# ScalarE's layer evictions move behind the next step's count eviction

## The chip, the cores and the metric

The kernel runs on one core of a Trainium2 chip. Its time is the device time of one execution in microseconds. The engines are named as in the profile: PE is TensorE's matmuls and PEld its weight loads, ACT is ScalarE, DVE is VectorE, POOL is GpSimd, SP is SyncE. Each engine runs its own instructions in their written order, and the engines wait for one another through signals (semaphores).

## What is computed

A wide-and-deep recommender for 16384 rows: mean word embeddings of 32 tokens, mean embeddings of three features of 20 ids each, four single ids, a wide sum, and a network of three layers with ReLU.

```python
tok = word_emb[token_idx].mean(axis=1)
e1 = emb_mh1[mh1_idx].mean(axis=1)
...
o4 = emb_oh4[oh4_idx]
emb = jnp.concatenate([tok, e1, e2, e3, o1, o2, o3, o4], axis=1)
...
h = jax.nn.relu(emb @ W1 + b1)
h = jax.nn.relu(h @ W2 + b2)
h = jax.nn.relu(h @ W3 + b3)
return jax.nn.sigmoid(h @ Wd + bd + wide)
```

The layers are 748 to 1024, to 512, to 256, and to 1.

## The kernel before

The batch is cut into 128 tiles of 128 rows. A tile takes 11 steps (`STEPS`), and the main loop (L528) runs over all steps, 1408 and 16 more at the end for what is left (`WAKE`). The order of the work on every engine is the order in which this loop writes it.

**Counts.** The small features are not gathered. DVE makes one-hot rows of the ids (`one_hots`, L291; tiles `row` and `slice`), for the step after the current one. PE multiplies them in `counts` (L307): 12 matmuls a step, 8 in a tile's last, into the PSUM tile `pc`, of which there is one. ACT evicts `pc` into `cnt` (L324). PE can't start the next step's counts before that eviction has ended.

**Sums.** In the tile after, `small_sums` (L332) multiplies `cnt` with the tables: some 15 matmuls a step into `pg`, right behind the step's counts. DVE reduces `pg` into `g` (L348).

**Tokens.** POOL gathers the word embeddings, two rows of each batch row at a time (`tokens`, L222; tile `tok_rows`, 8 buffers), 4096 indirect transfers. DVE adds them up (`add_up`, L210; lines L214 to L220). POOL can issue the next gather into a buffer when DVE has added the one before.

**Transposes.** When a tile's sums or tokens are complete, PE transposes them (`add_small`, L380, and `add_tokens`, L394) into a PSUM tile `pt`, and DVE copies `pt` into the layers' input. In the loop the transposes stand right behind the step's counts.

**Layers.** `mlp` (L432) runs on two tiles of rows at a time. Each layer's output is cut into tiles of 128 columns: `layer` (L414) adds up one such tile in PSUM (`ph`) with 6, 8 or 4 matmuls, and ACT evicts it with ReLU into `h` (L428). At the end come the output row `po` (L444) and the sigmoid. `mlp` is a generator: at each step's end `Paced.to` (L461) takes from it as many matmuls as are due, about four. So a `ph` may be begun in one step and finished in another, and the step that finishes one often begins the next. `ph`, `pt`, `po` and `pk` (the transposed ids, L282) share two PSUM buffers (`ps_h`); a new tile takes the buffer that was given back first.

A step writes its work in this order: one-hots, counts and their eviction, transposes, token adds, sums, layers.

Of the kernel before, what the change touches and what calls it, by code (L numbers as in the profile page):

```python
# [13 lines left out]
AF = mybir.ActivationFunctionType  # L14
# [17 lines left out]
STEPS = -(-HALF // ONEHOT)  # L32
# [16 lines left out]
def kernel(  # L49
# [21 lines left out]
    nc = tc.nc  # L71
# [7 lines left out]
    for f in SMALL:  # L79
        n = -(-tables[f].shape[0] // P)  # L80
# [210 lines left out]
    def one_hots(sc, s, i):  # L291

        b = i * ONEHOT
        rows = min(ONEHOT, HALF - b)
        row1 = ohp.tile([P, ONEHOT, P], BF16, name="row1")
        slice1 = ohp.tile([P, ONEHOT, n_h], BF16, name="slice1")
        for w, (one, n) in enumerate(((row1, P), (slice1, n_h))):
            shape = [P, rows, n // 2, 2]
            nc.vector.tensor_tensor(  # L299
                one[:, 0:rows, :].rearrange("p i (n d) -> p i n d", d=2),  # L300
                iota[:, 0:n].rearrange("p (n d) -> p n d", d=2).unsqueeze(1).to_broadcast(shape),
                sc[:, s // 2, w, s % 2, b : b + rows, :].unsqueeze(2).to_broadcast(shape),
                ALU.is_equal,
            )
        return row1, slice1

    def counts(cnt, hot, i):  # L307

        b = i * ONEHOT
        rows = min(ONEHOT, HALF - b)  # L310
        n = rows // 2
        pc = ps_c.tile([P, 2, 2, 512], F32, name="pc")
        for k in range(rows):
            for f in range(2):
                half = slice(f * HALF, (f + 1) * HALF)
                at = k % n * n_h
                nc.tensor.matmul(  # L317
                    pc[:, f, k // n, at : at + n_h],
                    hot[0][half, k, :],
                    hot[1][half, k, :],  # L320
                    start=True,
                    stop=True,
                )
        nc.scalar.activation(  # L324
            cnt[:, :, b : b + rows, :].rearrange("l f (g k) h -> l f g (k h)", g=2),
            pc[:, :, :, 0 : n * n_h],
            AF.Copy,
            scale=0.5,
            saturate=False,
        )  # L330
# [36 lines left out]
    class Block:  # L367
# [42 lines left out]
        def chunk(self, k):  # L410
            x = self.small[:, k, :] if k < 4 else self.tok[:, k - 4, :]
            return x[: chunk_k[k], 0 : self.n]

    def layer(dst, weights, bias, srcs, n_out):  # L414
        n = srcs[0].shape[-1]
        for m in range(n_out):
            ph = ps_h.tile([P, N], F32, name="ph", tag="ph")
            for k, src in enumerate(srcs):
                nc.tensor.matmul(  # L419
                    ph[:, 0:n],  # L420
                    weights[: src.shape[0], k, m * P : (m + 1) * P],
                    src,
                    start=(k == 0),
                    stop=(k == len(srcs) - 1),
                )
                if k < len(srcs) - 1:
                    yield 1
            nc.scalar.activation(dst[:, m, 0:n], ph[:, 0:n], AF.Relu, bias=bias[:, m : m + 1])  # L428
            yield 1
        yield None  # L430

    def mlp(block):  # L432


        n = block.n
        h1 = hp.tile([P, M1, N], F32, name="h1", tag="odd")
        yield from layer(h1, w1_sb, b1_sb, [block.chunk(k) for k in range(NK)], M1)
        h2 = hp.tile([P, M2, N], F32, name="h2", tag="even")
        yield from layer(h2, w2_sb, b2_sb, [h1[:, k, 0:n] for k in range(M1)], M2)
        h3 = hp.tile([P, M3 + 1, N], F32, name="h3", tag="odd")  # L440
        yield from layer(h3, w3_sb, b3_sb, [h2[:, k, 0:n] for k in range(M2)], M3)
        po = ps_h.tile([1, N], F32, name="po", tag="ph")
        for k in range(M3):
            nc.tensor.matmul(  # L444
                po[:, 0:n], wd_sb[:, k : k + 1], h3[:, k, 0:n], start=(k == 0), stop=(k == M3 - 1)
            )
        y = h3[0:1, M3, 0:n]
        nc.vector.tensor_add(y, po[:, 0:n], block.wide[:, 0:n])
        nc.scalar.activation(y, y, AF.Sigmoid, bias=bd_sb)
        b0 = block.first * P  # L450
        nc.sync.dma_start(out=out[b0 : b0 + n, :].rearrange("n o -> o n"), in_=y)
        yield M3
# [44 lines left out]
    tiles = B // P  # L497
# [26 lines left out]
    tables_on_chip = Paced(tables_on_chip)  # L524
    sc = key_columns(lookup_keys(ix))
    hot = one_hots(sc, 0, 0)
    layers, before, g = None, None, None
    for step in range(n_steps):  # L528
        t, i = divmod(step, STEPS)
        s = t % NSUB  # L530
        if i == 0:
            if g is not None:
                wide_term(g)
                waiting.append((step + 1, Block.add_small, t - 2, g))
            sums = g = None
            if 1 <= t <= tiles:
                g = gp.tile([P, G_COLS], F32, name="g")
                sums = sums_by_step(small_sums(g, cnt))
            if t < tiles:
                if s == 0 and t:  # L540
                    sc = next_sc
                cnt = cp.tile([P, 2, HALF, n_h], FP8, name="cnt", tag="counts")
        if t < tiles:
            hot_now = hot
            if s == 1 and i == 0 and t + NSUB < tiles:
                ix = load_indices(t // NSUB + 1)
            if s == 2 and i == 0 and t + NSUB < tiles + 1:
                next_keys = lookup_keys(ix)
            if i < STEPS - 1:
                hot = one_hots(sc, s, i + 1)  # L550
            elif t + 1 < tiles:
                hot = one_hots(next_sc if s == NSUB - 1 else sc, (s + 1) % NSUB, 0)
            counts(cnt, hot_now, i)
            tables_on_chip.to(TABLE_PACE * (step - 2))
            if t == 1 and i == STEPS - 1:
                load_weights()
        if waiting and step >= waiting[0][0]:
            block = transpose(*waiting.pop(0)[1:])
            if block:
                if layers:  # L560
                    layers.finish()
                layers = Paced(mlp(block), LAYER_TIME * block.n / P)
                last = block.first + block.n // P
                begin, left = step, (ready(ends[last] - 1) if last < tiles else n_steps) - step
        known = set(sums_of)
        toks.to(n_all * (step + 1) / n_steps)
        for k in set(sums_of) - known:
            waiting.append((step + 2, Block.add_tokens, k, sums_of.pop(k)))
        if s == 2 and i == 1 and t + NSUB < tiles + 1:
            next_sc = key_columns(next_keys)  # L570
        ahead = 0
        if sums:
            done = next(sums)
            ahead = n_h * (i + 1) / STEPS - done
        if layers:
            layers.to(mlp_work * layers.size * (step + 1 - begin) / left + ahead)
# [43 lines left out]
```

## Time and profile before

| | before |
|---|---|
| median of 3 runs (lowest to highest) | 7639.67 us (7632.0 to 7650.83) |
| the profiled execution | 7640.41 us, span 7638.6 us |
| mean granted clock of TensorE | 0.875 |
| busy share PE, PEld, DVE, ACT, POOL | 78%, 61%, 51%, 34%, 51% |

In the rows of the profile a number behind `x` counts instructions. In a timeline row stand the start in the span, the busy time, the engine, line and operation, what it writes and reads, and in brackets how long the engine was idle before and what ended that. In a row of waits stand who waited for whom, the total, how many times, and the longest. `remote` is a wait that no instruction in the trace ends, and `issue` is time in which the engine waited for nothing that the profile shows. In a row of windows stand the stretch, its length, the busy time of each engine with its instructions, the granted clock, the share of DMA and GB/s. In a group's row stand the busy time, the mean in ns, and the idle time before.

### The profile page before, as it was taken

Reading aid. Unit: us, or ns where it says so; the run is one execution under the profiler, and the core shown is the slowest. Engines: PE = TensorE matmul, PEld = TensorE weight load, DVE = VectorE, ACT = ScalarE, POOL = GpSimd, SP = SyncE. Lnnn points to the kernel's source line nnn. Section 1 sums busy time; section 2 is a strip of 40 time slices with the busy share of each in tenths; the row PEclk is TensorE's granted clock in tenths of the full one; section 3 lists DMA queues with packets and bytes.
Section 4 is the critical chain, followed back from the end, with each engine's and each line's share of the span. In section 5 each row is a group of like instructions: output and inputs, shape, how many; then the busy total and the mean of one; then the engine's idle time right before and its main releaser. Section 6 shows DMA issues by size and latency. Waiting matters only on the chain.

```text
span 7638.6 us, 116204 instructions
## 1 busy us (share of the span) xinstructions
PE 5965.6 (78%) x46772; PEld 4692.2 (61%) x46772; DVE 3907.9 (51%) x8513; ACT 2574.7 (34%) x2403; POOL 3887.3 (51%) x4103
## 2 busy tenths in 40 slices
PE   4777777877777787877888888777778777777778
PEld 3656666666656666666666666666666666666667
DVE  6544454455544555545555555555545545454543
ACT  4333333333333333333333333333333333333332
POOL 6544454454554455555555555555555545444543
PEclk8888888888988888888888889898888988888889
DMA  5333333333333333333333333333333333333322
GB/s 147 86 81 84 82 84 82 83 86 82 84 84 83 82 86 86 83 86 84 88 88 85 88 87 90 88 86 86 87 85 86 87 81 83 81 81 82 85 80 64
DMA packets 253003, 653.37 MB, mean 86 GB/s; under 512 B 119040, under 2 KB 119617, under 8 KB 252461
## 3 DMA queue, kind: packets, MB, share of 16 engines
q0 software_dynamic: 196608, 629.41, 30.4%
q1 hardware_dynamic: 55853, 16.53, 1.0%
q8 instruction: 366, 6.00, 0.3%
q14 instruction: 176, 1.44, 0.1%
HBM read 645.59 MB, written 0.07 MB: 85 GB/s over the span
## 4 chain that ended last, share of the span: by engine, by line
PE 52%; another core or an unknown queue 19%; DVE 14%; issue 11%; ACT 4%; DVEq 0%; SPq 0%; DMA 0%; ACTq 0%
PE ph L419 24%; PE pg L342 17%; PE pc L317 8%; DVE own L216 4%; ACT cnt L324 4%; DVE slice L299 3%; DVE own L220 3%; DVE row L299 1%; PE po L444 1%; PE pt L387 1%; ACT h L428 1%; PE pt L403 1%; DVE g L348 0%; PE pt L384 0%
## 5 line engine op out<-in xcount | busy, mean ns | idle before, releaser
L232 POOL DMA_INDIRECT tok_rows<-in_word_emb_dram,it x4096 | 3886.4, 949 | 3711.7 <-DVE own L220 2388.0
L324 ACT ACTIVATE cnt<-pc 128x1656 fp8e3<-128x1656 f32 (+1 forms) x1408 | 2123.6, 1508 | 3163.7 <-remote 1568.4
L342 PE MATMUL pg<-terms,cnt 128*128 128x195 bf16 x17664 | 2187.3, 273 | 454.9 <-issue 394.1
L342 PEld LDWEIGHTS <-cnt 128*128 128x128 fp8e3 x17664 | 1805.4, 147 | 730.6 <-issue 612.7
L299 DVE TENSOR_TENSOR row<-own,sc 128x768 bf16<-128x768 bf16 (+1 forms) x1408 | 763.1, 542 | 1828.6 <-remote 1349.5
L317 PE MATMUL pc<-slice,row 64*128 64x138 bf16 x16384 | 824.6, 236 | 865.6 <-ACT cnt L324 336.1
L419 PE MATMUL ph<-h,w_sb 128*128 128x256 f32 (+1 forms) x5200 | 1395.8, 411 | 97.6 <-issue 90.4
L317 PEld LDWEIGHTS <-row 64*128 64x128 bf16 x16384 | 575.3, 100 | 1373.0 <-issue 1183.0
L419 PE MATMUL ph<-x_small,w_sb 128*128 128x256 f32 (+3 forms) x4160 | 1203.8, 418 | 85.2 <-issue 66.3
L419 PEld LDWEIGHTS ph<-h,w_sb 128*128 128x128 f32 x5200 | 1021.8, 210 | 277.9 <-issue 146.7
L428 ACT ACTIVATE h<-ph,b_sb 128x256 f32<-128x256 f32 (+1 forms) x910 | 427.6, 470 | 1813.5 <-remote 859.3
L419 PEld LDWEIGHTS ph<-x_small,w_sb 128*128 128x128 f32 (+1 forms) x4160 | 827.1, 213 | 236.9 <-issue 120.4
L216 DVE TENSOR_TENSOR own<-own,tok_rows 128x300 f32<-128x300 f32 x1920 | 917.0, 478 | 63.1
L348 DVE TENSOR_REDUCE g<-pg 128x130 f32<-128x390 f32 (+1 forms) x512 | 261.5, 511 | 1232.2 <-remote 515.9
L220 DVE TENSOR_TENSOR own<-own,tok_rows 128x300 f32<-128x300 f32 x1792 | 857.1, 478 | 61.8
L299 DVE TENSOR_TENSOR slice<-own,sc 128x828 bf16<-128x828 bf16 (+1 forms) x1408 | 797.0, 566 | 0.0
L419 PE MATMUL ph<-x_tok,w_sb 128*128 128x256 f32 (+1 forms) x2080 | 624.6, 407 | 23.1 <-issue 22.2
L419 PEld LDWEIGHTS ph<-x_tok,w_sb 128*128 128x128 f32 x2080 | 409.9, 209 | 88.0 <-issue 36.6
L405 DVE TENSOR_SCALAR x_tok<-pt 128x256 f32<-128x256 f32 x128 | 54.3, 424 | 338.3 <-PE pt L404 269.3
L388 DVE TENSOR_TENSOR x_small<-pt,scale 128x384 f32<-128x384 f32 x128 | 70.9, 554 | 104.3 <-PE pt L387 84.3
L444 PE MATMUL po<-h,wd_sb 128*1 128x256 f32 (+1 forms) x260 | 89.3, 470 | 37.4 <-ACT h L428 25.4
L403 PE MATMUL pt<-ident,g_tok 128*128 128x128 f32 x256 | 59.8, 316 | 28.1 <-ACT h L428 22.5
(43 smaller groups left out, 805.4 us busy)
## 6 DMA issues: line engine op xcount, KB each, us to landing
tok_rows<-in_word_emb_dram,it POOLq DMA_INDIRECT x4096
ix<-in_idx_dram SPq DMA_DIRECT2D x128, 32.0 KB
w_sb<-in_W_dram SPq DMA_DIRECT2D x6, 512.0 KB
raw<-in_mh_dram SPq DMA_DIRECT2D x3, 747.5 KB
it<-in_idx_dram SPq DMA_DIRECT2D x32, 64.0 KB
w_sb<-in_W_dram SPq DMA_DIRECT2D x1, 2048.0 KB
out_dram<-h SPq DMA_DIRECT2D x63, 1.0 KB
raw<-in_mh_dram SPq DMA_DIRECT2D x1, 617.5 KB
```

Of the source, the lines that this page charges most:

```text
L216: nc.vector.tensor_add(tok_sum, tok_sum, a)
L220: nc.vector.tensor_add(to, tok_sum, b)
L232: nc.gpsimd.indirect_dma_start(out=rows[:, r * TOK_D : (r + 1) * TOK_D], out_offset=None, in_=word, in_offset=bass.IndirectOffsetOnAxis(ap ...
L299: nc.vector.tensor_tensor(one[:, 0:rows, :].rearrange("p i (n d) -> p i n d", d=2), iota[:, 0:n].rearrange("p (n d) -> p n d", d=2).unsque ...
L317: nc.tensor.matmul(pc[:, f, k // n, at : at + n_h], hot[0][half, k, :], hot[1][half, k, :], start=True, stop=True,)
L324: nc.scalar.activation(cnt[:, :, b : b + rows, :].rearrange("l f (g k) h -> l f g (k h)", g=2), pc[:, :, :, 0 : n * n_h], AF.Copy, scale=0 ...
L342: nc.tensor.matmul(pg[:, j, :], by_slice[:, :, h], terms[:, h, :], start=(h == h0), stop=(h == h1 - 1))
L348: nc.vector.tensor_reduce(g[:, at : at + n * ROW].rearrange("p (f d) -> p f d", f=n), pg[:, 0:n, :].rearrange("p f (c d) -> p f d c", c=3) ...
L403: nc.tensor.transpose(pt[:, k, :], g[:, k * P : (k + 1) * P], ident)
L419: nc.tensor.matmul(ph[:, 0:n], weights[: src.shape[0], k, m * P : (m + 1) * P], src, start=(k == 0), stop=(k == len(srcs) - 1),)
L428: nc.scalar.activation(dst[:, m, 0:n], ph[:, 0:n], AF.Relu, bias=bias[:, m : m + 1])
L444: nc.tensor.matmul(po[:, 0:n], wd_sb[:, k : k + 1], h3[:, k, 0:n], start=(k == 0), stop=(k == M3 - 1))
```

## The change

A finished layer tile is no longer evicted at once. `evict_later` notes it, and `evict` writes the noted eviction behind the next step's count eviction. It is written earlier where another tile is finished before that, so that at most one is noted; where a layer has ended and the generator goes on; and at the end, once all counts are written. Since PE runs in order, a count eviction that has waited for its counts has waited for every layer matmul ahead of them as well, and the layer's eviction behind it needs no signal of its own: of PE's 3259 instructions that signal, 2397 are left. The matmuls keep their order and number on PE, and so does the work of DVE, POOL and SP.

```diff
--- before.py
+++ after.py
@@ -411,6 +411,21 @@
             x = self.small[:, k, :] if k < 4 else self.tok[:, k - 4, :]
             return x[: chunk_k[k], 0 : self.n]
 
+    unevicted = []
+
+    def evict():
+        for dst, ph, bias in unevicted:
+            nc.scalar.activation(dst, ph, AF.Relu, bias=bias)
+        unevicted.clear()
+
+    def evict_later(*what):
+
+
+        evict()
+        unevicted.append(what)
+        if counted == tiles:
+            evict()
+
     def layer(dst, weights, bias, srcs, n_out):
         n = srcs[0].shape[-1]
         for m in range(n_out):
@@ -425,9 +440,10 @@
                 )
                 if k < len(srcs) - 1:
                     yield 1
-            nc.scalar.activation(dst[:, m, 0:n], ph[:, 0:n], AF.Relu, bias=bias[:, m : m + 1])
+            evict_later(dst[:, m, 0:n], ph[:, 0:n], bias[:, m : m + 1])
             yield 1
         yield None
+        evict()
 
     def mlp(block):
 
@@ -524,7 +540,7 @@
     tables_on_chip = Paced(tables_on_chip)
     sc = key_columns(lookup_keys(ix))
     hot = one_hots(sc, 0, 0)
-    layers, before, g = None, None, None
+    layers, g, counted = None, None, 0
     for step in range(n_steps):
         t, i = divmod(step, STEPS)
         s = t % NSUB
@@ -551,6 +567,8 @@
             elif t + 1 < tiles:
                 hot = one_hots(next_sc if s == NSUB - 1 else sc, (s + 1) % NSUB, 0)
             counts(cnt, hot_now, i)
+            evict()
+            counted = t + (i == STEPS - 1)
             tables_on_chip.to(TABLE_PACE * (step - 2))
             if t == 1 and i == STEPS - 1:
                 load_weights()
```

The lines from L414 on move by 15 to 18; the layer's eviction is L418, the layer's matmul L434 and the output row's L460. What stands on ACT at one place in the middle of the program, the first layer of a block (`h1` from `ph` is a layer's eviction, `cnt` from `pc` a count eviction; the numbers tell the tiles apart and shift by one in the changed kernel; in brackets whose signals an instruction waits for), before:

```order
L324 ACTIVATE cnt_19669<-pc_20145 128x2x552 [waits PE_49]
L428 ACTIVATE h1_19772<-ph_20135,b1_sb_133 128x256 [waits PE_49]
L324 ACTIVATE cnt_20175<-pc_20180 128x2x828 [waits PE_49]
L428 ACTIVATE h1_19772<-ph_20165,b1_sb_133 128x256 [waits PE_49]
L324 ACTIVATE cnt_20175<-pc_20232 128x2x828 [waits PE_49]
L428 ACTIVATE h1_19772<-ph_20224,b1_sb_133 128x256 [waits PE_49]
L324 ACTIVATE cnt_20175<-pc_20283 128x2x828 [waits PE_49]
```

and after the change:

```order
L324 ACTIVATE cnt_19668<-pc_20144 128x2x552 [waits PE_49]
L418 ACTIVATE h1_19772<-ph_20056,b1_sb_133 128x256
L324 ACTIVATE cnt_20174<-pc_20179 128x2x828 [waits PE_49]
L418 ACTIVATE h1_19772<-ph_20134,b1_sb_133 128x256
L324 ACTIVATE cnt_20174<-pc_20231 128x2x828 [waits PE_49]
L418 ACTIVATE h1_19772<-ph_20164,b1_sb_133 128x256
L324 ACTIVATE cnt_20174<-pc_20282 128x2x828 [waits PE_49]
```

Every layer eviction has moved behind one more count eviction and has lost its wait for PE: that of `ph_20165` stood ahead of the eviction of `pc_20232`, and as `ph_20164` it stands behind that of `pc_20231`, the same tile.

What stands on PE at that place, from the end of these counts to the first sums, before:

```order
L317 LDWEIGHTS row1_20176
L317 MATMUL pc_20232<-slice1_20177,row1_20176 128x138
L384 MATMUL pt_20246<-ident_103,g_19668 128x128 [waits Activation_49]
L387 MATMUL pt_20246<-ident_103,g_19668 128x128 x3
L342 LDWEIGHTS cnt_19669
L342 MATMUL pg_20259<-terms_128,cnt_19669 128x195 [waits DVE_49]
```

and after the change:

```order
L317 LDWEIGHTS row1_20175
L317 MATMUL pc_20231<-slice1_20176,row1_20175 128x138
L384 MATMUL pt_20246<-ident_103,g_19667 128x128 [waits Activation_49]
L387 MATMUL pt_20246<-ident_103,g_19667 128x128 x3
L342 LDWEIGHTS cnt_19668
L342 MATMUL pg_20259<-terms_128,cnt_19668 128x195 [waits DVE_49]
```

PE's rows are the same, and nothing has moved on it. The transpose waits for ACT in both, since it takes the buffer of the layer tile that was finished just ahead of these counts (`ph_20165`, now `ph_20164`). But the eviction that gives this buffer back now stands behind the eviction of the counts right above the transpose.

## The prediction

> **What bounds the kernel now.** I read the page first, then the waits by engine, then single steps in order of time.
>
> ```profile
> span 7638.6 us, 116204 instructions
> PE 5965.6 (78%) x46772; PEld 4692.2 (61%) x46772; DVE 3907.9 (51%) x8513; ACT 2574.7 (34%) x2403; POOL 3887.3 (51%) x4103
> PE 52%; another core or an unknown queue 19%; DVE 14%; issue 11%; ACT 4%; DVEq 0%; SPq 0%; DMA 0%; ACTq 0%
> ```
>
> TensorE (PE) looks like the bound, but 19% of the chain is time that no instruction of another engine ends, on a kernel of one core. Two stretches of the trace show that PE's work alone doesn't set the pace. The first pair of rows counts the count matmuls (128 per batch tile), the second all engines.
>
> ```profile
> 117.10:172.70 55.60, 7.61 (x128) 16.60 (x11) 0.71 0.34 92
> 231.80:7500.00 7268.20, 789.22 (x15804) 2047.89 (x1358) 0.88 0.31 84
> 117.10:172.70 55.60, 29.71 (x277) 24.68 (x277) 31.77 (x72) 16.60 (x11) 30.33 (x33) 0.71 0.34 92
> 231.80:7500.00 7268.20, 5733.01 (x44886) 4495.50 (x44886) 3727.44 (x8130) 2451.22 (x2280) 3700.21 (x3911) 0.88 0.31 84
> ```
>
> In the first stretch no layer runs yet: one tile takes 55.6 us with PE busy for 29.7. Afterwards 7268.2 x 128 / 15804 = 58.9 us per tile, with PE busy for 5733.0 x 128 / 15804 = 46.4: 16.7 us more PE work costs 3.3 (the granted clock was 0.71 and 0.88, so the work differs by rather more). So something else has the larger say. The waits:
>
> ```profile
> ACT cnt L324 <- remote: 1568.4, 292, 12.1
> ACT h L428 <- remote: 859.3, 153, 12.1
> POOL tok_rows L232 <- DVE own L220: 2388.0, 666, 17.1
> PE pc L317 <- ACT cnt L324: 336.1, 142, 10.4
> ```
>
> ScalarE (ACT) waits 1568 us for counts and 859 us for layers with no visible end. One such place, in order of time:
>
> ```profile
> 5672.13 0.54 PE L317 MATMUL pc<-slice,row 64*128 64x138 bf16 x12
> 5673.55 0.94 POOL L232 DMA_INDIRECT tok_rows<-in_word_emb_dram,it  x1 [0.30 <-issue]
> ...
> 5674.60 0.09 PEld L317 LDWEIGHTS <-row 64*128 64x128 bf16 x1 [0.33 <-issue]
> ...
> 5678.55 0.95 POOL L232 DMA_INDIRECT tok_rows<-in_word_emb_dram,it  x1 [0.30 <-issue]
> 5680.23 1.55 ACT L324 ACTIVATE cnt<-pc 128x1656 fp8e3<-128x1656 f32 x1 [9.76 <-remote]
> ...
> 5681.76 0.47 ACT L428 ACTIVATE h<-ph,b_sb 128x256 f32<-128x256 f32 x1
> 5681.83 0.88 PE L317 MATMUL pc<-slice,row 64*128 64x138 bf16 x12 [7.16 <-ACT cnt L324]
> ...
> 5685.49 0.94 POOL L232 DMA_INDIRECT tok_rows<-in_word_emb_dram,it  x1 [5.99 <-DVE own L214]
> ```
>
> The counts were done at 5672.67 and ACT was idle, yet it began at 5680.23: PE's signal came 7.5 us late, while GpSimd (POOL) issued gathers back to back (0.30 us between them). It came once POOL had nothing left to issue (from 5679.5 to 5685.49). PE then stood 7.16 us. So the kernel is bound by a loop: gathers hold PE's signals back, the late signals hold ACT and VectorE (DVE), DVE frees the gather buffers late (POOL's 2388 us).
>
> **What the change removes.** 862 of 3259 signals, nearly all a layer tile's (ph). What matters is what stands behind one:
>
> ```profile
> 5133.75 0.38 PE L419 MATMUL ph<-x_small,w_sb 128*128 128x256 f32 x1
> 5134.06 0.36 PEld L317 LDWEIGHTS <-row 64*128 64x128 bf16 x12 [0.33 <-issue]
> 5135.78 0.47 ACT L428 ACTIVATE h<-ph,b_sb 128x256 f32<-128x256 f32 x1 [3.26 <-PE pc L317]
> 5137.83 0.09 PEld L317 LDWEIGHTS <-row 64*128 64x128 bf16 x1 [0.33 <-issue]
> 5138.71 1.55 ACT L324 ACTIVATE cnt<-pc 128x1656 fp8e3<-128x1656 f32 x1 [2.46 <-remote]
> 5140.31 0.55 PE L317 MATMUL pc<-slice,row 64*128 64x138 bf16 x12 [2.42 <-DVE own L216]
> ```
>
> The layer ended at 5134.1, the counts at 5134.6, but the layer's signal arrives at 5135.78 and the counts' only 2.93 us later. Without the layer's signal the counts' could have had its place: the eviction ends at 5137.33, and PE, whose next weights are in at 5137.83, goes on there and not at 5140.31. That is 2.48 us, 0.85 of the gap. I went through ACT's rows from 187 to 7250 us for steps whose count signal is still out when a layer's arrives; the first and the last are
>
> ```profile
> 188.80 0.47 ACT L428 ACTIVATE h<-ph,b_sb 128x256 f32<-128x256 f32 x1 [2.45 <-PE pc L317]
> 193.09 1.55 ACT L324 ACTIVATE cnt<-pc 128x1656 fp8e3<-128x1656 f32 x1 [3.81 <-remote]
> ...
> 7233.02 0.48 ACT L428 ACTIVATE h<-ph,b_sb 128x256 f32<-128x256 f32 x1 [2.53 <-remote]
> 7235.37 1.55 ACT L324 ACTIVATE cnt<-pc 128x1656 fp8e3<-128x1656 f32 x1 [1.88 <-remote]
> ```
>
> There are 233, with 420 us between the two signals in all; in 110 the two come together. 0.85 x 420 = 357 us; in the 110 the count eviction also no longer stands behind a layer eviction of 0.47 us; as the two signals come some 0.1 us apart, I take 0.35 us each, 40 us. Gain: 400 us. Its ends: nothing, if the counts' signal just takes the place as the one held; 859 us, all that ACT waits for late layers.
>
> A signal that isn't held costs PE nothing that I can see: the counts' weights follow a finished layer tile (5674.60) and an unfinished one (5137.83) after the same 0.33 us.
>
> **What it adds.** The layer's eviction (Relu) now stands behind the next step's count eviction. It issues nothing else, adds no instruction, and no DMA queue is passed. But it gives a PSUM buffer (there are two) and its part of h back later. Behind it in PE's order wait transposes (pt), the output row (po) and the next layer tile but one. Before, with signals on time:
>
> ```profile
> 5688.76 0.47 ACT L428 ACTIVATE h<-ph,b_sb 128x256 f32<-128x256 f32 x1 [4.46 <-PE ph L419]
> 5689.03 0.54 PE L317 MATMUL pc<-slice,row 64*128 64x138 bf16 x12
> 5689.50 0.44 PE L403 MATMUL pt<-ident,g_tok 128*128 128x128 f32 x2
> 5689.61 1.55 ACT L324 ACTIVATE cnt<-pc 128x1656 fp8e3<-128x1656 f32 x1 [0.38 <-PE pc L317]
> 5690.09 0.42 DVE L405 TENSOR_SCALAR x_tok<-pt 128x256 f32<-128x256 f32 x1 [3.78 <-PE pt L404]
> ```
>
> The Relu ends at 5689.23, ahead of the transpose at 5689.50. After the change it would run at 5691.16 to 5691.63, and the transpose wait 2.1 us, with the sums and layers queued on PE behind it. The durations and today's waits:
>
> ```profile
> L324 ACT ACTIVATE cnt<-pc 128x1656 fp8e3<-128x1656 f32 (+1 forms) x1408 | 2123.6, 1508 | 3163.7 <-remote 1568.4
> L428 ACT ACTIVATE h<-ph,b_sb 128x256 f32<-128x256 f32 (+1 forms) x910 | 427.6, 470 | 1813.5 <-remote 859.3
> PE pt L384 <- ACT h L428: 23.4, 16, 3.4
> PE pt L403 <- ACT h L428: 22.5, 12, 4.6
> DVE x_tok L405 <- PE pt L404: 269.3, 92, 25.4
> ```
>
> Following the two buffers through the new order, 102 of the 256 groups of transposes take one whose Relu stands behind the count eviction of their own step. 102 x (1.51 + 0.47 + 0.1) = 212 us. Is it on the path? DVE already waits for 92 of the 128 token transposes, so I take 92 / 128: 153 us. 49 of 65 output rows stand there too, mostly behind transposes that wait as well: by 2.08 less some 0.9 us for those, 59 us. 206 layer tiles start after the step's sums (about 1.5 us of PE work as cover) on such a buffer: 0.4 us each, 80 us; with late signals up to 1.5 us each. Layer boundaries need the Relu only at their last chunk, some matmuls on: nothing, at most 35 us. Cost: about 300 us. From above: 212 + 206 x 1.5 + 49 x 1.5 + 35 = 630. From below: if PE work costs only 3.3 / 16.7 of itself, as in the two stretches, 60.
>
> At this point a rule speaks against the change: the Trainium skill, PSUM — Partial Sum Buffer, in its summary of rules, asks to evacuate PSUM promptly because it is tight. The trace agrees as far as it goes (46 us of waits at transposes with prompt Relus); no run here shows a late one. By that rule alone the sum would be 7640 + 300, without the gain.
>
> The profiled execution took 7640.41 us, 1.8 over its span and 0.01% from the median of 7639.67, so the sum goes for the median: 7640 - 400 + 300 = **7540 us**, 1.3% faster.
>
> **The rivals.**
> - *PE waits for the late Relus* (slower). The 357 places (102 + 206 + 49) cost in full what late count signals add to them, 520 us, and the gain halves to 200, since a counts' signal at the head is often held too (5680.23 above, with no layer ahead of it): 7960 us. For it: the transposes come right after the counts, where nothing covers. Against it: the 3.3 us for 16.7 us of PE work. It decides from a mean of 400 / 357 = 1.1 us per place on. Chance 0.34, from just above no change to that price.
> - *The gathers set the time* (no change). Signals arrive when POOL runs dry, whatever their number, and the Relu waits hide in the same idle time: 7640. For it: 5680.23. Against it: 5135.78, where one signal came and the next didn't. Chance 0.10.
> - *Each signal has a small fixed price.* Serialized one after another, 862 fewer save the same little each: by the equal 0.33 us rows zero, at most a tenth of that, 28 us: 7612 to 7640. Beside it: the Trainium skill, TensorE: Matmul & The Clock Gate, on the per-tile semaphore tail, fits 26.3 ns per increment; an estimate by it is 862 x 26.3 ns = 23 us, 7617. The trace does not show such a step. Chance 0.04.
> - *The loop loosens.* Fewer held signals free gather buffers sooner, all 859 us go, and PE pays the 300: 7080 us. Chance 0.10.
>
> **How the numbers follow.** The forecast has 0.42, with a range of its own from 7380 to 7615 (gain or cost off by 100 to 150). A measurement of this kernel can tell about 0.3%, 23 us. Faster: 0.42 + 0.10 = 0.52. Same: 0.10 + 0.04 = 0.14. Slower: 0.34. Cases of both signs hold most of the chance; 7300 to 7880 leaves out about 0.08 of the loosened loop and 0.10 of the waiting PE.
>
> **What would show it.** Right: ACT's 859 us of waits for layers vanish, its wait without visible end for counts grows by less than they fall, PE's wait of 336 us for the count eviction and POOL's 2388 shrink, and new rows of PE transposes waiting for h show 100 to 250 us. Wrong: those rows, with po and ph, hold over 400 us; POOL's wait grows; or the count signals come as late as before, with no layer's signal ahead of them.

## The result

| | before | after |
|---|---|---|
| median (lowest to highest) | 7635.84 us (7626.6 to 7650.83), 4 runs | 8033.53 us (8029.74 to 8044.8), 4 runs |
| the profiled execution | 7640.41 us | 8035.36 us |
| mean granted clock of TensorE | 0.875 | 0.864 |

The ratio is 1.0521, with a 95% interval from 1.0501 to 1.0542: 398 us slower. The forecast was 7540, and its range ended at 7880. Ratios, here and below, are stated with their 95% intervals; they are not the quotients of the medians, which differ from them by up to 0.3% and lie within the intervals. One execution of the kernel that is late only at its transposes (below) took 10318.68 us at a granted clock of 0.55 and is left out.

The page of the changed kernel, its span, busy times and chain:

```profile
span 8033.6 us, 116243 instructions
PE 6099.2 (76%) x46772; PEld 4762.6 (59%) x46772; DVE 3911.7 (49%) x8513; ACT 2519.1 (31%) x2403; POOL 3899.5 (49%) x4103
PE 45%; another core or an unknown queue 23%; DVE 14%; issue 11%; ACT 8%; DVEq 0%; SPq 0%; DMA 0%; ACTq 0%
```

The part of the chain that nothing visible ends grew from 19% to 23%, and ACT's from 4% to 8%. PE's own work didn't become the bound. The waits of the changed kernel:

```profile
ACT cnt L324 <- remote: 2829.1, 423, 12.4
POOL tok_rows L232 <- DVE own L220: 2782.0, 682, 17.7
ACT cnt L324 <- PE pc L317: 1999.4, 851, 9.8
DVE x_tok L405 <- PE pt L404: 416.3, 109, 26.0
PE pc L317 <- ACT cnt L324: 281.2, 107, 11.9
PE ph L434 <- ACT h L418: 156.1, 67, 8.7
PE pt L403 <- ACT h L418: 128.2, 48, 5.6
PE pt L384 <- ACT h L418: 126.3, 52, 5.0
PE po L460 <- DVE wide_row L392: 84.1, 35, 4.9
ACT h L418 <- remote: 29.2, 4, 9.2
```

ACT's wait for layers (859.3 us before) is gone, as the change intends. It has moved: ACT now waits 2829.1 us instead of 1568.4 for counts without a visible end. The two groups of ACT's evictions, of the changed kernel:

```profile
L324 ACT ACTIVATE cnt<-pc 128x1656 fp8e3<-128x1656 f32 (+1 forms) x1408 | 2124.9, 1509 | 5258.4 <-remote 2829.1 <-PE pc L317 1999.4 <-PE pg L342 275.5
L418 ACT ACTIVATE h<-ph,b_sb 128x256 f32<-128x256 f32 (+1 forms) x910 | 423.1, 465 | 115.6 <-PE ph L434 86.3 <-remote 29.2
```

Before, ACT was idle 3163.7 + 1813.5 = 4977.2 us ahead of the two, now 5258.4 + 115.6 = 5374.0. That is 396.8 us more, about the loss itself. POOL's wait for DVE (L220) grew by 2782.0 - 2388.0 = 394.0. The engines are busy for nearly as long as before, so the lost time has to show as idle time on each of them; the rows tell on which waits it falls.

What a late Relu does, in order of time, in the changed kernel:

```profile
2997.07 0.54 PE L317 MATMUL pc<-slice,row 64*128 64x138 bf16 x12
2997.39 0.95 POOL L232 DMA_INDIRECT tok_rows<-in_word_emb_dram,it  x1 [0.30 <-issue]
2999.39 1.55 ACT L324 ACTIVATE cnt<-pc 128x1656 fp8e3<-128x1656 f32 x1 [3.87 <-remote]
3000.84 0.47 ACT L418 ACTIVATE h<-ph,b_sb 128x256 f32<-128x256 f32 x1
3001.36 0.20 PEld L403 LDWEIGHTS pt<-ident,g_tok 128*128 128x128 f32 x2 [3.93 <-ACT h L418]
3001.36 0.44 PE L403 MATMUL pt<-ident,g_tok 128*128 128x128 f32 x2 [3.75 <-ACT h L418]
3001.95 0.42 DVE L405 TENSOR_SCALAR x_tok<-pt 128x256 f32<-128x256 f32 x1 [6.41 <-PE pt L404]
```

The counts end at 2997.61 and no layer's signal stands ahead of theirs, yet ACT begins only at 2999.39, 1.78 us later: the signal is held all the same. Then the Relu starts 1.45 us after the count eviction, PE's transposes wait 3.75 us for its buffer, and DVE, which takes the transposes before it adds the gathered rows, waits 6.41.

### The profile page after: what moved, and what is told of

It is laid out like the page before. It is cut to its first block, busy times and chain, and to the rows that moved or that the text cites. A ratio compares the mean times of both kernels' runs of the same rounds, so it can differ in the third digit from the quotient of the medians.

```text
span 8033.6 us, 116243 instructions
## 1 busy us (share of the span) xinstructions
PE 6099.2 (76%) x46772; PEld 4762.6 (59%) x46772; DVE 3911.7 (49%) x8513; ACT 2519.1 (31%) x2403; POOL 3899.5 (49%) x4103
## 3 DMA queue, kind: packets, MB, share of 16 engines
q0 software_dynamic: 196608, 629.41, 29.2%
## 4 chain that ended last, share of the span: by engine, by line
PE 45%; another core or an unknown queue 23%; DVE 14%; issue 11%; ACT 8%; DVEq 0%; SPq 0%; DMA 0%; ACTq 0%
PE ph L434 20%; PE pg L342 14%; PE pc L317 7%; ACT cnt L324 7%; DVE own L216 4%; DVE slice L299 4%; DVE own L220 3%; PE po L460 1%; ACT h L418 1%; DVE row L299 1%; PE pt L387 1%; PE pt L403 1%; PE pt L384 0%; DVE g L348 0%
## 5 line engine op out<-in xcount | busy, mean ns | idle before, releaser
L232 POOL DMA_INDIRECT tok_rows<-in_word_emb_dram,it x4096 | 3898.6, 952 | 4095.5 <-DVE own L220 2782.0
L324 ACT ACTIVATE cnt<-pc 128x1656 fp8e3<-128x1656 f32 (+1 forms) x1408 | 2124.9, 1509 | 5258.4 <-remote 2829.1
L342 PE MATMUL pg<-terms,cnt 128*128 128x195 bf16 x17664 | 2222.0, 277 | 404.4 <-issue 365.3
L342 PEld LDWEIGHTS <-cnt 128*128 128x128 fp8e3 x17664 | 1839.9, 147 | 679.4 <-issue 558.9
L434 PE MATMUL ph<-h,w_sb 128*128 128x256 f32 (+1 forms) x5200 | 1410.3, 413 | 136.8 <-issue 100.9
L434 PE MATMUL ph<-x_small,w_sb 128*128 128x256 f32 (+3 forms) x4160 | 1253.2, 432 | 225.2 <-ACT h L418 134.2
L434 PEld LDWEIGHTS ph<-h,w_sb 128*128 128x128 f32 x5200 | 1020.9, 210 | 332.3 <-issue 156.8
L434 PEld LDWEIGHTS ph<-x_small,w_sb 128*128 128x128 f32 (+1 forms) x4160 | 848.0, 220 | 410.2 <-ACT h L418 162.4
L220 DVE TENSOR_TENSOR own<-own,tok_rows 128x300 f32<-128x300 f32 x1792 | 857.2, 478 | 61.9
L434 PE MATMUL ph<-x_tok,w_sb 128*128 128x256 f32 (+1 forms) x2080 | 632.2, 411 | 14.6 <-issue 13.6
L434 PEld LDWEIGHTS ph<-x_tok,w_sb 128*128 128x128 f32 x2080 | 420.3, 214 | 84.2 <-issue 26.3
L418 ACT ACTIVATE h<-ph,b_sb 128x256 f32<-128x256 f32 (+1 forms) x910 | 423.1, 465 | 115.6 <-PE ph L434 86.3
L460 PE MATMUL po<-h,wd_sb 128*1 128x256 f32 (+1 forms) x260 | 97.2, 502 | 108.5 <-DVE wide_row L392 84.1
L403 PE MATMUL pt<-ident,g_tok 128*128 128x128 f32 x256 | 63.9, 335 | 132.4 <-ACT h L418 128.2
```

Of the source, the lines that this page charges most:

```text
L220: nc.vector.tensor_add(to, tok_sum, b)
L232: nc.gpsimd.indirect_dma_start(out=rows[:, r * TOK_D : (r + 1) * TOK_D], out_offset=None, in_=word, in_offset=bass.IndirectOffsetOnAxis(ap ...
L324: nc.scalar.activation(cnt[:, :, b : b + rows, :].rearrange("l f (g k) h -> l f g (k h)", g=2), pc[:, :, :, 0 : n * n_h], AF.Copy, scale=0 ...
L342: nc.tensor.matmul(pg[:, j, :], by_slice[:, :, h], terms[:, h, :], start=(h == h0), stop=(h == h1 - 1))
L403: nc.tensor.transpose(pt[:, k, :], g[:, k * P : (k + 1) * P], ident)
L418: nc.scalar.activation(dst, ph, AF.Relu, bias=bias)
```

## The experiments

**Two theories.** Theory 1: the gathers hold PE's signals, however many signals there are, so fewer signals bring nothing, and the late Relus cost about 400 us. Theory 2, the prediction's: fewer signals bring some 400 us, so the late Relus cost the measured loss and that gain together.

The runs came in five groups, each compared with the kernel before on its own chip. The kernel before took 5191.6 us in the first, 7655.3 in the second, 7639.9 in the third, 5192.0 in the fourth, 7529.3 in the fifth: on the chip of the first group PE's signals are hardly held (0.21 us late on average in the kernel with 852 more of them, 1.96 in the trace of before), and the fourth group's chip is taken to be of the same kind by its time. So ratios and differences are compared, and the expectations in absolute numbers of the first group, written for a kernel before of 7640 us, can only be read so.

"Late" below is the time from the end of the signalling matmul to the rise of its semaphore, both listed in the trace; the matmul's end is modelled. A few per cent of the signals have no partner in that list and are left out.

### Signals put back

The changed kernel, with a signal behind each layer tile's last matmul again, to an empty instruction of SP that nothing waits for:

```diff
+    def signal(mm):
+        nop = nc.sync.nop()
+        tc.add_manual_dep(nop.ins, mm.ins.name, ...)
...
-                nc.tensor.matmul(
+                mm = nc.tensor.matmul(
...
+            signal(mm)
             evict_later(dst[:, m, 0:n], ph[:, 0:n], bias[:, m : m + 1])
```

> The changed kernel, and the last matmul of every layer tile signals again, for a no-op on SyncE that waits for it and does nothing: PE gives 3365 signals instead of 2397, and nothing else moves. Theory 1 (a count signal is held by the gathers whatever stands ahead of it, and the 400 us come from layer evictions that free PSUM late): as the changed kernel, 8030 us, within 30. Theory 2 (a layer's signal ahead does hold the counts' signal up; the change saved this and lost more than it by the late evictions): slower than the changed kernel by what the change saved, up to 400 us: 8200 to 8430.

Measured: 5650.32 us against 5191.63, ratio 1.0885 (1.0867 to 1.0904). So with every signal in place the late Relus cost 459 us there. The changed kernel itself did not run on this chip, so this run alone doesn't decide between the theories. The kernel before with 852 signals more, from each layer tile's last but one matmul, in the same way:

> The kernel before, and the last matmul but one of every layer tile signals too, for a no-op on SyncE: PE gives 4111 signals instead of 3259, the evictions stay where they were. Theory 1: as the kernel before, 7636 us, within 30. Theory 2: another 852 signals cost what 862 fewer should have saved, up to 400 us: 7800 to 8040.

Measured: 5191.73 us, ratio 0.9999 (0.999 to 1.0009). On this chip 852 signals cost nothing. Whether they do where they are held was tried in the second group, the changed kernel beside the one with its signals put back:

> The changed kernel itself, beside the runs that change one part of it. Theory 1 (the late Relus cost time, fewer signals bring nothing): where the kernel before takes about 5190 us, the ratio is that of the kernel with the signals put back, 1.085 to 1.092, so 5630 to 5670 us; where the kernel before takes about 7636 us, the ratio is 1.05 again. Theory 2 (each signal less is worth time, and the late Relus cost more than the sum of both): the changed kernel is clearly below the kernel with the 806 signals put back, by over 1% of its time, on whichever chip.

> The changed kernel with a signal behind the last matmul of each of a layer's outputs again. Theory 1: within 0.5% of the changed kernel of the same call. Theory 2: over 1% above it; where PE's signals are held (the kernel before at about 7636 us) some 400 us above it, by the prediction's term for the count signals that stood behind a layer's.

Measured: 8052.95 us (ratio 1.0546, 1.0514 to 1.0578) and 8082.65 us (1.0561, 1.0529 to 1.0593), against 7655.26. The second has 3365 - 2397 = 968 signals more (not the 806 of the expectation). The two differ by 30 us or 0.4%, and their intervals overlap; theory 2 asked for some 400. It falls: what the missing signals bring lies between nothing and some tens of us.

### Late only at the transposes, and late everywhere else

The first of the two kernels leaves the Relu late only where the next step has transposes (150 signals fewer than before), the second only elsewhere (700 fewer). Each is a line or two of the changed kernel:

```diff
-        if counted == tiles:
+        if counted == tiles or not (waiting and step + 1 >= waiting[0][0]):
             evict()
```

```diff
             layers.to(mlp_work * layers.size * (step + 1 - begin) / left + ahead)
+        if waiting and step + 1 >= waiting[0][0]:
+            evict()
```

On the chip of the first group:

> The changed kernel, but a layer's eviction moves behind the next count eviction only where that step has a transpose; elsewhere it is issued at once, as before. 150 evictions are late, and PE gives 3109 signals. Theory 1: it carries the transposes' and output rows' part of the loss. The waits of PE for ScalarE's layer evictions at transposes grew by 229 us of some 390 in all (275 after, 46 before), so 7636 + 200 to 270: 7840 to 7910. If PE's waits there were idle time anyway: 7640.

> The changed kernel, but a layer's eviction is issued ahead of the next count eviction where that step has a transpose; elsewhere it stays late. 162 evictions are prompt, and PE gives 2559 signals. Theory 1: only the waits of later layer tiles and output rows are left, 7636 + 100 to 200: 7740 to 7840; together with the kernel that is late there alone, the two losses add to some 398 us. Theory 2 (fewer signals save up to 400 us once the worst waits are gone): below 7600.

Measured: 5551.97 us, ratio 1.0697 (1.0679 to 1.0714), and 5257.23 us, ratio 1.0127 (1.011 to 1.0143), so 360 and 66 us; 200 to 270 and 100 to 200 were expected. In the third group, where signals are held:

> The changed kernel, late only at the steps whose end has a batch of transposes, 150 layers' outputs; all others at once. The prediction's term for these was 153 us, on a kernel before of 7640 us. Theory 1 as the runs on the chip with prompt signals have it (2.4 us for each late one): ratio 1.04 to 1.05, 300 to 380 us above the kernel before, most of the whole loss. Rival (with held signals the transposes cost only what the prediction took, and po and ph waits the rest): 100 to 200 us, ratio 1.013 to 1.026.

> The changed kernel with its Relus at once where transposes follow, late everywhere else (all that is left is the prediction's terms for po and ph, 139 us, and its gain for the signals, 400 us). Theory 1 (no gain, po and ph cost little): ratio 1.005 to 1.02, 40 to 150 us above the kernel before. The prediction's gain, if it is there at all and was only covered by the transposes: 200 us or more below the kernel before.

Measured: 7943.25 us (three runs), ratio 1.0409 (1.0385 to 1.0432), and 7709.52 us, ratio 1.0098 (1.0081 to 1.0115), against 7639.85: 303 and 70 us, together 373 of the loss of 398. The waits of the first of them, late at the transposes:

```profile
POOL tok_rows L232 <- DVE own L220: 2686.6, 673, 18.0
DVE x_tok L405 <- PE pt L404: 391.4, 106, 26.3
PE pt L384 <- ACT h L418: 131.6, 52, 5.7
PE pt L403 <- ACT h L418: 131.1, 48, 6.2
PE po L460 <- DVE wide_row L392: 88.6, 36, 4.6
```

and of the second:

```profile
POOL tok_rows L232 <- DVE own L220: 2449.4, 669, 16.5
PE ph L434 <- ACT h L418: 152.3, 70, 7.0
DVE x_tok L405 <- PE pt L404: 285.3, 96, 24.9
```

100 groups of transposes that wait are most of the loss. PE's waits at them are 131.6 + 131.1 = 263 us, against 46 in the kernel before; with the output rows' 89 us, for which the kernel before has no row, that is 305 us more, as much as the kernel lost. A wait of the same kind and of 152 us in sum, at layer tiles, costs less than half of itself. The likely reason is that the step's sums ahead of it and the layer's matmuls behind it leave DVE its work; no run isolates that. The second kernel has 700 signals fewer than the kernel before and few late transposes, and still gains nothing.

### Half of the gathers

One gather of each pair is left out, and the row that is there is added twice, so that PE, ACT and DVE keep their work and the token sums come from half of the rows:

```diff
-        a, b = rows[:, 0:TOK_D], rows[:, TOK_D : 2 * TOK_D]
+        a = b = rows[:, 0:TOK_D]
...
-                for r in range(TOK_GROUP):
+                for r in range(1):
```

> The kernel before with one gather of each pair left out (2048 instead of 4096); the row that is there is added twice, so DVE, ACT and PE do the same work and the token sums come from half of the rows. Theory 1 with the gathers as what holds PE's signals: where the kernel before takes 7636 us, this falls to 5100 to 6200 us, and the row of waits of ACT cnt for a remote releaser, 1568 us of before, to under 400. If something else holds the signals it stays above 7000 us. Where the kernel before takes 5190 us, this comes to 4900 to 5150 us, with PE as what sets the time.

> The changed kernel with one gather of each pair left out in the same way. Theory 1: the late Relus make PE wait whatever POOL does, so this lies 300 to 500 us above the half-gather kernel of this call that has the Relus at once. Rival (the cost is made of the gathers: POOL and DVE run dry because a step is longer, and with gathers to spare it goes): within 100 us of it.

Measured, where the kernel before takes 7655 us: 5195.63 us, ratio 0.6796 (0.6772 to 0.682), and 5634.92 us, ratio 0.737 (0.7344 to 0.7396). The busy times of the kernel before with half of the gathers, from its page:

```profile
PE 5073.8 (98%) x46772; PEld 4161.9 (80%) x46772; DVE 3907.1 (75%) x8513; ACT 2593.6 (50%) x2403; POOL 1944.7 (37%) x2055
```

and its wait without a visible end, from its waits:

```profile
ACT cnt L324 <- remote: 10.6, 4, 4.1
```

PE is busy for 98%, and ACT's wait without a visible end has fallen from 1568 to 10.6 us. So on this chip the gathers held PE's signals. With half of them the kernel is as fast as the kernel before with all of its gathers on the chip of the first group, 5191.63 us. But gathers without a pause between them are not enough to hold a signal. On the chip of the first group, in the kernel with 852 signals more, POOL issues them like this:

```profile
L232 POOL DMA_INDIRECT tok_rows<-in_word_emb_dram,it x4096 | 3891.6, 950 | 1263.3 <-issue 853.5 <-DVE own L220 110.5 <-DVE own L216 92.0
```

All 4096 fall into six runs with no more than 0.75 us between two gathers, and yet the count signals are 0.21 us late on average.

The two kernels with half of the gathers also show the price of the Relus by themselves. The busy times of the changed kernel with half of the gathers:

```profile
PE 5208.5 (92%) x46772; PEld 4226.5 (75%) x46772; DVE 3909.4 (69%) x8513; ACT 2518.7 (45%) x2403; POOL 1944.8 (35%) x2055
```

and PE's waits in it:

```profile
PE pt L384 <- ACT h L418: 106.8, 53, 2.2
PE pt L403 <- ACT h L418: 96.7, 49, 2.2
PE po L460 <- DVE wide_row L392: 47.3, 36, 2.4
PE ph L434 <- ACT h L418: 36.5, 50, 0.9
```

5634.92 - 5195.63 = 439 us with the gathers out of the way, so the rival that gathers make the cost falls too. PE's waits in these rows are 287 us (3 in the kernel before with half of the gathers); the same 46772 matmuls take 5208.5 - 5073.8 = 135 us longer, at a granted clock of 0.98 instead of 0.997 (1.7% of these 2.7%). Together that is some 420 of the 439.

### What of a gather holds a signal

With half a row for each gather, from a table cut in two, so other data; the pair makes one row, which is added twice:

```diff
-                        out=rows[:, r * TOK_D : (r + 1) * TOK_D],
+                        out=rows[:, r * TOK_D // 2 : (r + 1) * TOK_D // 2],
...
-                        in_=word,
+                        in_=word.rearrange("v (h d) -> (v h) d", h=2),
```

> The kernel before with 4096 gathers of half a row each (rows of a table cut in two, so other data; the pair fills one row, which is added twice). The number of gathers, their issue and their packets stay, the bytes are halved. If the issue of the gathers holds the signals: within 3% of the kernel before (where that takes about 7640 us). If their transfers hold them: 5190 to 6500 us. Where the kernel before takes about 5190 us: no change, within 1%.

Measured: 7620.76 us, ratio 0.9973 (0.9961 to 0.9985). Its row of the gathers' queue:

```profile
q0 software_dynamic: 196608, 314.83, 17.9%
```

The bytes are half (629.41 MB in the kernel before) and the packets the same. So it is not the bytes; whether it is the gathers themselves or their packets, this run can't tell, since both keep their number.

Four buffers for gathered rows instead of 8 (`TOK_BUFS = 4`):

> The kernel before with 4 buffers for gathered rows instead of 8, so that POOL can be at most one pair of gathers ahead of what DVE adds and long runs of gathers issued back to back cannot form. Where the kernel before takes about 7640 us. Theory 1 (PE's signals are held while four or more gathers are issued one behind the other): the runs get shorter, the row of waits of ACT cnt for a remote releaser (1568 us in before) falls under 700, and the time falls to 5600 to 7200 us. Rival (POOL is then too little ahead of DVE, and its waits take the place of the held signals): 7600 to 8300 us. Where the kernel before takes about 5190 us: 5200 to 5900 us, since only the second can act there.

Measured: 7644.83 us, ratio 1.0004 (0.9988 to 1.002). No change, but it tells nothing of theory 1: the gathers with no more than 0.75 us between them still come in runs of 6.3 on average (6.2 before). The buffers don't set the length of a run.

Pauses on POOL, iotas into a tile that nobody reads, after every, every second or every fourth gather (here two after every second):

```diff
+    pause = const.tile([P, 270], I32, name="pause")
...
+                for _ in range(2):
+                    nc.gpsimd.iota(pause, pattern=[[1, 270]], base=0, channel_multiplier=0)
```

> The kernel before with an iota of 128x270 on POOL (about 0.36 us by the kernel's own iota, 128x138 in 0.233 us) behind every gather, into a tile that nobody reads: no gather follows another at once, and POOL's own work is about 4096 x 1.61 = 6600 us. Theory 1 (PE's signals are held while gathers are issued back to back): where the kernel before takes about 7640 us the signals come promptly and the time falls to 6650 to 7100 us. Rival (the number of gathers in a stretch of time holds them, or 0.4 us is no pause): 7500 us or more. Where the kernel before takes about 5190 us: 6600 to 6800 us, POOL being the pace.

> The same sum of pauses, two such iotas behind every second gather. Theory 1 with the held signals beginning at the third gather of a run, as the trace of before shows it: as good as a pause behind each gather, 6650 to 7100 us. If any two gathers in a row hold the signals: clearly above the kernel with the pause behind each.

> The same sum of pauses, four such iotas behind every fourth gather. Theory 1: signals are held in the third and fourth gather of each run and come in the pause, 1.4 us; so the time lies above the kernel with a pause behind each pair, 6900 to 7500 us, but below the kernel before where that takes 7640 us. If only the sum of POOL's work counts: the same as the other two.

> One iota of 128x220 (about 0.31 us) behind every second gather: POOL's own work is about 5120 + 2048 x 0.31 = 5760 us. Theory 1: if 0.3 us is pause enough for a held signal to go through, 5800 to 6500 us; if not, 7300 us or more.

This group fell on a chip on which the kernel before takes 5192 us: 6165.01 (1.1875, 1.1855 to 1.1895), 6996.81 (1.3477, 1.3454 to 1.3499), 6947.07 (1.338, 1.3358 to 1.3403) and 5566.56 us (1.0722, 1.0704 to 1.074). So they give the price of a pause only, and don't tell the theories apart. The first was expected at 6600 to 6800 us on such a chip and came out below. The rows of POOL, pauses behind each gather, and then two behind each second:

```profile
L233 POOL DMA_INDIRECT tok_rows<-in_word_emb_dram,it x4096 | 3890.5, 950 | 687.8 <-issue 597.4 <-DVE row L301 52.4 <-DVE own L221 10.9
L239 POOL IOTA pause<- 128x270 int32 x4096 | 1518.0, 371 | 36.2
```

```profile
L233 POOL DMA_INDIRECT tok_rows<-in_word_emb_dram,it x4096 | 3879.8, 947 | 1444.2 <-issue 1316.5 <-DVE own L217 37.1 <-DVE x_small L409 33.1
L240 POOL IOTA pause<- 128x270 int32 x4096 | 1479.2, 361 | 161.7
```

The same 4096 iotas cost 973 us behind single gathers and 1805 behind pairs, since POOL's `issue` time falls in the one and grows in the other (597.4 and 1316.5 us, against 853.5 in the row without pauses above). The last two runs, the short pause again, and one of 128x64 behind every gather, fell on a chip with held signals:

> The kernel before with one iota of 128x220 behind every second gather, which took 5566.6 us, POOL being the pace, on a chip where the kernel before takes 5192 us. Where the kernel before takes about 7640 us. Theory 1 (gathers issued back to back hold PE's signals there, a pause of 0.33 us lets them through): 5560 to 6500 us, faster than both kernels. If so short a pause does not help: 7300 us or more. Where the kernel before takes about 5190 us: 5560 to 5570 us again.

> The kernel before with an iota of 128x64 behind every gather: by the rows of the runs before it the iota takes about 0.16 us and the 0.30 us behind a gather shrinks to 0.16 us, so that POOL's work comes to about 4096 x 1.28 = 5240 us. Where the kernel before takes about 5190 us: 5220 to 5320 us. Where the kernel before takes about 7640 us. Theory 1, if any other instruction between two gathers lets the signals through: 5250 to 6300 us; if a stretch without issue of at least some tenths of a us is needed: within 3% of the kernel before.

Measured: 7278.01 us, ratio 0.966 (0.962 to 0.9699), and 7407.13 us, ratio 0.9846 (0.9829 to 0.9862), against 7529.27. The first is 3.4% faster than the kernel before, and so than both kernels, on that chip; where signals are not held it is 7.2% slower. Its largest waits:

```profile
POOL tok_rows L233 <- DVE own L221: 1606.4, 508, 10.3
ACT cnt L326 <- remote: 1263.6, 290, 10.6
```

They are smaller than before (2388.0 and 1568.4), and most of the loop is still there, with count signals 1.7 us late on average. Theory 1 had 5560 to 6500 for it. That a pause of 0.33 us lets a held signal through is not so, or only in part. The second stays within the 3% that its expectation has for a pause too short to help.

## Why the prediction was wrong

**The step that failed is the gain**: "Without the layer's signal the counts' could have had its place", 0.85 of 420 us and 40 us more, together 400. The runs show none of it clear of the noise: 968 signals put back change the time by 30 us, and the kernel with 700 signals fewer and few late transposes is 70 us slower than the kernel before.

The trace's times of PE's signals show what became of it. In before, 259 of some 1365 count signals were still out when a layer's arrived ahead of them (the prediction counted 233), and these were 4.81 us late on average, the others 1.29. In after there are 2 such, and all are 1.95 us late on average, as in before (1.96). With the signals put back 199 stand behind a layer's again, 4.76 us late, and the mean of all is 1.77. So a layer's signal ahead of a late one marked a stretch in which signals were held; it was not what held them. What held them goes with the gathers: in before a count signal that fell into the third or a later gather of a run, or the 0.75 us behind it, was 3.9 us late, in the first two 0.4, with POOL idle 0.1; in after 3.6, 0.7 and 0.1. The prediction had read this at its first example (5680.23, a signal 7.5 us late with no layer ahead), and had named nothing as one end of the gain ("if the counts' signal just takes the place as the one held"). It then took the other end's reading from one instance (5135.78) and multiplied it by 233. The number of pairs was about right; that removing one of two late signals makes the other early was never in a row.

**The cost was mis-sized**, 300 us where the runs show 373 to 398.

- Transposes and output rows: 153 + 59 = 212 us, measured 303. The number of places was right: 102 by the order, 52 + 48 in the trace. The wait of one was right as well: 126.3 + 128.2 - 45.9 = 208.6 us more on PE, against 102 x 2.08 = 212. Wrong was to take 92 / 128 of it as on the path, because DVE waited there before: the waits count in full. The output rows were put at 59 us and wait 84.1 for the buffer that DVE has not yet read. A likely reason for the full count is the order on DVE, which takes the transposes ahead of the token adds that free POOL's buffers, so that a later transpose makes DVE, POOL and the next gathers later too. POOL's wait grew with it (2388.0 to 2686.6 us where only these Relus are late), but no run takes that link out alone.
- Layer tiles: 206 x 0.4 = 80 us, measured 70 where only the late Relus away from the transposes are left. Right in sum, by luck: the places at which PE is seen to wait are fewer and dearer, 70 times 2.2 us, and less than half of these 152 us counts.
- A signal that isn't held costs PE nothing: right. 852 more of them on a PE that is busy for 98% give a ratio of 0.9999, on the chip of the first group.

The Trainium skill, TensorE: Matmul & The Clock Gate, on the per-tile semaphore tail, fits 26.3 ns for each increment; an estimate by it is 852 x 26.3 ns = 22 us, and the interval around 0.9999 leaves 5. That tail doesn't show in this run.

The rule that was weighed against the change, to evacuate PSUM promptly (the Trainium skill, PSUM — Partial Sum Buffer, summary of rules), was the better guide: 150 evictions that come one count eviction later cost 303 to 360 us.

**Of the rivals** "PE waits for the late Relus" has the sign and the mechanism; its price of 7960 had a cost of 520 and a gain of 200, where the runs show some 400 and no gain clear of the noise; that 7960 lies nearest to the 8034 measured is in part luck. "The gathers set the time" was right in that the signals come as late whatever their number, and wrong in that the Relu waits would hide in the time that the late signals leave idle. "The loop loosens" went the other way: POOL's wait grew.

**The signs named ahead** were right to split it: ACT's waits for layers vanished, but its wait for counts grew by 1261 us where they fell by 830; POOL's grew; pt, ph and po together waited 126.3 + 128.2 + 156.1 + 84.1 = 495 us; the count signals came as late as before. Only two of the signs for right came true: the waits for layers that vanished, and PE's wait for the count eviction, which shrank from 336.1 to 281.2. The new rows at the transposes, 254.5 us, end just above their 100 to 250. All three signs for wrong came true.

**Open.** Why gathers hold PE's signals, and why on some chips only, is not settled. The runs show, on the chips where signals are held, that it goes by the number of gathers or of their packets and not by their bytes, that half of them hold next to nothing (count signals 0.13 us late on average), and that ACT's and DVE's waits follow. That it takes gathers issued without anything between them is argued from the lateness by place in a run; on the chip of the first group far longer runs of gathers hold next to nothing (0.21 us), and on that of the fourth signals are late with pauses on POOL (below), so more than the gathers may play a part. The two pauses that were tried on a chip with held signals shorten the time by 3.4% and 1.5% and do not end it. Longer pauses were not run on such a chip.

## What to carry to other kernels

When a signal comes late, ask what holds it before counting what stands ahead of it: two late signals in a row can have a common cause, as here, and an experiment that thins out the suspected holder (here half of the gathers) shows it in one run. A wait that moves from one instruction to another has gained nothing until something ends sooner; here ACT's idle time tells it, 859 us of waits gone at one line and 1261 added at the next. Think twice before evicting a PSUM buffer behind a longer eviction if the next user of the buffer sits right behind it in TensorE's order: here those waits counted in full, 305 us of them for a loss of 303.

## What the runs showed of the hardware

- The same kernel took 7529 to 7655 us on some chips and 5192 on others. What differs is how late PE's signals are while POOL issues gathers: 1.96 us on average in the trace of before; 0.21 in the kernel with 852 signals more, where the kernel before takes 5192. ACT's and DVE's instructions last as long on both (1508 ns for a count eviction, 478 for a token add).
- On the chip of the fourth group, where the kernel before takes 5192 us, PE's signals were late with the longer pauses: 0.94 us on average with an iota behind each gather and 1.73 with two behind each pair, but 0.06 with the short one behind each pair. No run tells why.
- The granted clock was lower where PE was less busy: 0.997 at 98% (the kernel with half of the gathers), 0.98 at 92%, 0.864 at 76%. The share alone doesn't set it: with two pauses behind each pair of gathers it was 0.918 at 79%, with the short pause on a chip with held signals 0.889 at 80%. With more waits on PE the same matmuls took longer in sum: with half of the gathers that is 135 us of the 439, 2.7%, of which the clock explains 1.7%.
